# Column transforms in four array tiles at once, and a last stage with small chunks at both ends and four buffers

## The chip, the cores and the metric

The kernel runs on one core of a Trainium2 chip. A core has a tensor engine (PE; its weight loads are listed apart as PEld), a vector engine (DVE), a scalar engine (ACT), a general engine (POOL), a sync engine (SP) that here only issues transfers, and 16 DMA engines that move data between the device memory (HBM) and the on-chip buffer (SBUF). The tensor engine writes its results into PSUM, eight banks of 512 float32 values for each of 128 partitions; DVE and ACT copy ("evacuate") them to SBUF. The metric is the device time of one launch in microseconds. Before the change it is 1813.42 us, the median of three runs from 1812.36 to 1813.81. The profiled execution has a span of 1809.2 us, and all times of single instructions below are counted from its start.

## The reference, cut to what matters

The input is `x` of shape (4, 56, 56, 128), float32: four images of 3136 tokens with 128 channels. Layer 0 is a group norm, a 7x7 neighbourhood attention with four heads and a projection, added to `x`. Layer 1 adds an unnormalised attention over the tokens, and then a spectral unit: the normalised tokens are convolved along the sequence with 16 long filters (once plainly, once with alternating signs), and each filtered sequence goes through a 128x128 matrix of its own. Only one of four branches counts in the end, chosen by an argmax:

```
U = irfft(rfft(phi) * rfft(u))                  # 16 filters, plain and with signs
out = einsum('btkd,k,kde->bte', U, sigma**0.25, M)
t = t + out + (three short shifted products)
```

The change touches the way back from frequencies to tokens, and the sum into the output.

## The kernel before, in words

Everything is float32. `layers` does layer 0, layer 1's attention, the row half of the forward transform and the transforms of the filters; the change does not touch it. It leaves the current sum `t` in device memory as `td`, the row-transformed tokens as `xd`, and the filters' transforms as `vd`. A flag decides whether a second, general form of everything runs; with these inputs it does not.

`spectral_layer` then works frequency by frequency. The 3136 tokens are seen as a grid of 56 rows and 56 columns. The row transform gave N1 = 42 row frequencies `m1`; each holds a real and an imaginary part, two halves of the sequence (`NS` = 2, index `s`) and four images (`B`). Columns are split into even and odd ones (index `p`), so that a column transform is a product with a 56-row operand on partitions 0 to 55 for `p` = 0 and 64 to 119 for `p` = 1. The steps for one `m1` are:

- `token_points` (L1466): 16 products, 8 for each `p`, turn the tokens into 28 column frequencies, in one PSUM bank for each `p`: bank `px` of pool `ps_x`, and a bank of tag `g0`, shown as `xx`. DVE copies each bank to the tile `us` (L1481), ACT multiplies part of the same bank by -1 into `us` (L1482), POOL makes further copies (L1483 to L1485).
- `matrices` (L1487), eight calls `n` = 0 to 7: each fills four banks, `pg[0][0]`, `pg[0][1]`, `pg[1][0]`, `pg[1][1]`, of tags `g0`, `g1`, `g0`, `g1`, by 16 products of 32 rows. The four products of one round go to the four banks in this order. DVE evacuates the `g0` banks and ACT the `g1` banks into `gt` (L1505).
- `product` (L1510), seven calls: the frequency's tokens times its matrices, into `py`, evacuated as `ys`.
- `regroup` (L1524): `ys` goes to device memory as `yd` and comes back as `yg`, in the order that the inverse transform needs.
- `columns` (L1536): the inverse column transform, four products of 56x56 with 512 columns, one for each `s` and `p` (L1542). Each has a bank of its own, drawn in the order `g1`, `g0`, `g1`, `g0`. Four evacuations of 56x512 (L172 on ACT and L174 on DVE by turns) fill `zs`.
- `store_columns` (L1554): four transfers (L1556), one for each `p` and part, to `zd`, which is laid out column by column: `zd[w, part * 42 + m1, s, b, e]`.

The PSUM pool `ps_g` holds three banks for each of the tags `g0` and `g1`; a new tile of a tag takes one of its three banks, and the first instruction that writes it waits until the bank's last reader is done. The order of the tensor engine's instructions is as written (`manual_schedule`); the order on the other engines is picked by the framework's scheduler when the kernel is built. The loop runs `it` from -1 to 44 and works in a software pipeline: in pass `it` it interleaves `matrices` of frequency `it` with `product` of `it - 1`, and after the last of them come, in this order on the tensor engine, `token_points` of `it + 1` and `columns` of `it - 3`. Passes 3 to 40 (38 of them) have all four kinds of work.

`onto_the_rest` (L1600) is the last stage. For each of the 56 columns `w` it multiplies the 84 x 1024 values of `zd[w]` by a table `onto` (two accumulating products of 84x56 with 512 columns, L1625), multiplies by a mask and adds to `td` (DVE, L1634), and stores to the output. Columns `w` and `w + 28` (index `q`) go together, on the lower and upper half of the partitions. Seven chunks of `WC` = 4 column pairs are worked on, each with its transfers: `tl` from `td` (L1615, issued by ACT), `z` from `zd` (L1617, by SP, one for each `q`, 1344 KB), and the output (L1639, by ACT). The pool `fin` has three buffers of each, and its first transfers wait for the memory that the spectral pools give back. All `z` loads wait until the last `zd` store has landed, since every store touches every column.

Of the kernel before, what the change touches and what calls it, by code (L numbers as in the profile page):

```python
# [10 lines left out]
F32 = mybir.dt.float32  # L11
# [4 lines left out]
P = 128  # L16
B, H, W, C = 4, 56, 56, 128
# [39 lines left out]
NS, BR = 2, H // 2  # L57
N1, N2, NM = 42, W, W // 2
# [6 lines left out]
HALF = 2 * NM  # L65


def spectral_tables():

    m1 = np.arange(N1)  # L70
    m = m1[:, None] + N1 * np.arange(NM)[None]
    row = np.exp(-2j * np.pi * (m1[None] + 0.25) * np.arange(H)[:, None] / N1)
    rows = np.stack([row.real, row.imag], 1)
    into = np.zeros((P, 2 * N1))
    for g in range(NG):
        into[32 * g : 32 * g + BR] = rows[:BR].reshape(BR, -1)
    tok, back = np.zeros((2, N1, P, 2, NM))
    fil = np.zeros((N1, P, 2, NM, 2))
    for p in range(2):
        col = np.arange(p, N2, 2)  # L80

        fwd = np.exp(-2j * np.pi * (m[:, None, :] + 0.25) * col[None, :, None] / (2 * NP))

        bwd = np.exp(2j * np.pi * (m[:, :, None] + 0.25) * col[None, None, :] / (2 * NP)) / NP
        for part, turn in enumerate((1, 1j)):
            at = slice(64 * p + NM * part, 64 * p + NM * (part + 1))
            for to, a in ((tok, turn * fwd), (back, turn * bwd)):
                to[:, at] = np.stack([a.real, a.imag], 2)

            a = turn * fwd  # L90
            fil[:, 64 * part + NM * p : 64 * part + NM * (p + 1), p] = np.stack([a.real, a.imag], 3)

    onto = np.zeros((2, N1, NS, H))
    for s in range(NS):
        at = np.arange(H - BR * s)
        e = np.exp(2j * np.pi * (m1[:, None] + 0.25) * at[None] / N1)
        onto[0, :, s, BR * s :] = e.real
        onto[1, :, s, BR * s :] = -e.imag
    sign = np.ones((P, 1))
    sign[BR:N2] = sign[64 + BR : 64 + N2] = -1.0  # L100
    f = lambda a: np.ascontiguousarray(a, np.float32)
    return {
        "into": f(into),
        "taps_in": f(rows.reshape(H, -1)),
        "tok": f(tok.reshape(N1, P, -1).transpose(1, 0, 2)),
        "fil": f(fil.reshape(N1, P, -1).transpose(1, 0, 2)),
        "back": f(back.reshape(N1, P, -1).transpose(1, 0, 2)),
        "onto": f(onto.reshape(2 * N1, -1)),
        "sign": f(sign),
    }  # L110
# [13 lines left out]
def hybrid_kernel(  # L124
# [23 lines left out]
    nc = tc.nc  # L148
# [19 lines left out]
    def evacuate(dst, src):  # L168

        flip[0] ^= 1  # L170
        if flip[0]:
            nc.scalar.copy(dst, src)  # L172
        else:
            nc.vector.tensor_copy(dst, src)  # L174
# [1238 lines left out]
    def spectral_layer():  # L1413


        with ExitStack() as ph:
# [37 lines left out]
            def parts():  # L1454

                for p in range(2):
                    for part in range(2):
                        yield slice(64 * p + NM * part, 64 * p + NM * (part + 1)), p, part
# [77 lines left out]
            def columns(m1, yg, zs, pz):  # L1536

                back = tables_of(m1)[2]
                for s in range(NS):
                    for p in range(2):  # L1540
                        at = slice(64 * p, 64 * p + HALF)
                        nc.tensor.matmul(  # L1542
                            pz[s][p][at],
                            back[at],
                            yg[at, s * B : (s + 1) * B].rearrange("p k e -> p (k e)"),
                            start=True,
                            stop=True,
                        )
                for s in range(NS):
                    for p in range(2):  # L1550
                        at = slice(64 * p, 64 * p + HALF)
                        evacuate(zs[at, s], pz[s][p][at])

            def store_columns(m1, zs):  # L1554
                for at, p, part in parts():
                    nc.sync.dma_start(  # L1556
                        zd[p::2, part * N1 + m1].rearrange("w s b e -> w (s b e)"),
                        zs[at].rearrange("w s f -> w (s f)"),
                    )

            def bank(tag):
                if tag == "x":
# [6 lines left out]
            with tc.manual_schedule(engines={mybir.EngineType.PE}):  # L1569
                for it in range(-1, N1 + LAG):  # L1570
                    ap, az, au = it - 1, it - LAG, it + 1
                    if 0 <= it < N1:
                        gts[it] = sp.tile([P, 2, 2 * NM, C // 2, 2], F32, name="gt")
                        if it + 2 < N1:
                            xms[it + 2] = load_tokens(it + 2)
                    if 0 <= ap < N1:
                        ys = sp.tile([P, NM // 4, C], F32, name="ys")
                    if 0 <= az < N1:
                        zs = sp.tile([P, NS, B * C], F32, name="zs")
                    for n in range(8):  # L1580
                        if 0 <= it < N1:
                            matrices(it, gts[it], n)
                        if 0 <= ap < N1 and n < 7:
                            if n % 4 == 0:
                                py = ps_y.tile([P, 4, C], F32, name="py")
                            product(py, gts[ap], us2[ap % 2], n)
                            if n == 3 or n == 6:
                                evacuate(ys[:, n - n % 4 : n + 1], py[:, : n % 4 + 1])
                    if au < N1:
                        token_points(au, xms.pop(au), us2[au % 2], [bank("x"), bank("g0")])  # L1590
                    if 0 <= az < N1:
                        pz = [[bank(f"g{1 - p}") for p in range(2)] for s in range(NS)]
                        columns(az, ygs.pop(az), zs, pz)
                    if 0 <= ap < N1:
                        ygs[ap] = regroup(ap, ys)
                    if 0 <= az < N1:
                        store_columns(az, zs)
                    gts.pop(ap, None)

    def onto_the_rest():  # L1600

        with ExitStack() as ph:
            fin = ph.enter_context(tc.tile_pool(name="fin", bufs=3))
            ps_o = ph.enter_context(tc.tile_pool(name="ps_o", bufs=4, space=bass.MemoryType.PSUM))
            onto = fin.tile([2 * N1, NS, H], F32, name="onto", bufs=1)
            nc.sync.dma_start(onto, table["onto"].rearrange("p (s h) -> p s h", s=NS))
            rows_in = td.rearrange("b (h w) c -> h b w c", w=W)
            rows_out = ot.rearrange("b (h w) c -> h b w c", w=W)
            WC = 4
            for w0 in range(0, W // 2, WC):  # L1610
                tl = fin.tile([P, B, WC, C], F32, name="tl")
                zin = []
                for q in range(2):
                    ws = slice(q * BR + w0, q * BR + w0 + WC)
                    nc.scalar.dma_start(tl[64 * q : 64 * q + H], rows_in[:, :, ws])  # L1615
                    z = fin.tile([2 * N1, WC, NS, B * C], F32, tag=f"z{q}", name=f"z{q}")
                    nc.sync.dma_start(  # L1617
                        z, zd[ws].rearrange("w p s b e -> p w s (b e)")
                    )
                    zin.append(z)  # L1620
                for i in range(WC):
                    po = ps_o.tile([P, B, C], F32, name="po2")
                    for s in range(NS):
                        for q in range(2):
                            nc.tensor.matmul(  # L1625
                                po[64 * q : 64 * q + H].rearrange("p b c -> p (b c)"),
                                onto[:, s],
                                zin[q][:, i, s],
                                start=(s == 0),
                                stop=(s == NS - 1),  # L1630
                            )
                    for q in range(2):
                        at = slice(64 * q, 64 * q + H)
                        nc.vector.scalar_tensor_tensor(  # L1634
                            tl[at, :, i], po[at], hmask[at], tl[at, :, i], ALU.mult, ALU.add
                        )
                for q in range(2):
                    ws = slice(q * BR + w0, q * BR + w0 + WC)
                    nc.scalar.dma_start(rows_out[:, :, ws], tl[64 * q : 64 * q + H])  # L1639

    unfit = keep.tile([1, 1], mybir.dt.int32, name="unfit")
    layers(False, unfit)
# [61 lines left out]
```

## Time and profile before

| what | us |
| --- | --- |
| time, median of three | 1813.42 |
| span of the profile | 1809.2 |
| `layers` until the first token product (L1472) | 0 to 779.1 |
| spectral loop, first to last column evacuation's end | 779.1 to 1656.2 |
| one pass of the loop in its steady part (n = 0 of two passes: 1007.02 and 1027.35) | 20.33 |
| last stage, first `z` issue to the end | 1659.1 to 1809.2 |
| PE busy / DVE busy / ACT busy over the span | 1657.9 / 1070.5 / 756.3 |

A busy tensor engine in this profile is not one at its peak: matmuls are pipelined, their ends are modelled, and a short wait between two of them can be covered by the modelled end of the first. What a pass costs is therefore read from start times. In the slices of the page each digit is the busy share of one fortieth of the span, 45.2 us; the last three and a bit are the last stage, and the nineteen before them the loop.

### The profile page before, as it was taken

Reading aid. Unit: us, or ns where it says so; the run is one execution under the profiler, and the core shown is the slowest. Engines: PE = TensorE matmul, PEld = TensorE weight load, DVE = VectorE, ACT = ScalarE, POOL = GpSimd, SP = SyncE. Lnnn points to the kernel's source line nnn. Section 1 sums busy time; section 2 is a strip of 40 time slices with the busy share of each in tenths; the row PEclk is TensorE's granted clock in tenths of the full one; section 3 lists DMA queues with packets and bytes.
Section 4 is the critical chain, followed back from the end, with each engine's and each line's share of the span. In section 5 each row is a group of like instructions: output and inputs, shape, how many; then the busy total and the mean of one; then the engine's idle time right before and its main releaser. Section 6 shows DMA issues by size and latency. Waiting matters only on the chain. (4 is left out here: it accounts for less than half of the span.)

```text
span 1809.2 us, 71326 instructions
## 1 busy us (share of the span) xinstructions
PE 1657.9 (92%) x31481; PEld 1237.5 (68%) x31481; DVE 1070.5 (59%) x2142; ACT 756.3 (42%) x1529; POOL 390.3 (22%) x803
## 2 busy tenths in 40 slices
PE   4887898899999998779999999999999999995997
PEld 3665677567867766368888887888888887883221
DVE  4776786678868764135666666565666666562232
ACT  2333533366455444324444544454444544451000
POOL 4242254437446434000010001000000001000000
PEclk9788989899999997659999999999999999997555
DMA  6545446544343334632333333433434333325996
GB/s 166 116 88 106 86 94 147 121 119 124 88 136 91 92 98 112 198 92 65 99 106 105 96 87 100 113 99 88 102 104 107 89 91 97 103 72 150 239 226 182
DMA packets 285099, 207.69 MB, mean 115 GB/s; under 512 B 105868, under 2 KB 255532, under 8 KB 284652
## 3 DMA queue, kind: packets, MB, share of 16 engines
q1 hardware_dynamic: 275876, 189.50, 41.1%
q10 hardware_dynamic: 8904, 13.53, 2.7%
q8 instruction: 250, 4.10, 1.0%
q14 instruction: 69, 0.57, 0.1%
HBM read 115.31 MB, written 87.64 MB: 112 GB/s over the span
## 5 line engine op out<-in xcount | busy, mean ns | idle before, releaser
L1505 DVE COPY gt<-pg 128x448 f32<-128x448 f32 x672 | 388.4, 619 | 303.3 <-PE pg L1495 303.3
L1505 ACT COPY gt<-pg 128x448 f32<-128x448 f32 x672 | 326.0, 538 | 358.1 <-PE pg L1495 358.1
L1495 PE MATMUL pg<-v,mats 32*128 32x112 f32 x10752 | 402.2, 286 | 5.6 <-DVE gt L1505 2.0
L1495 PEld LDWEIGHTS pg<-v,mats 32*128 32x128 f32 x10752 | 341.8, 190 | 93.3 <-issue 51.7
L1514 PE MATMUL py<-gt,us 128*32 128x128 f32 x9408 | 339.2, 283 | 0.8 <-ACT ys L172 0.8
L1514 PEld LDWEIGHTS py<-gt,us 128*32 128x32 f32 x9408 | 266.9, 137 | 32.9 <-ACT ys L172 1.0
L1484 POOL COPY us<-us 128x448 f32<-128x448 f32 x42 | 23.4, 556 | 819.7 <-DVE us L1481 819.7
L1165 ACT ACTIVATE e<-scores 126x768 f32<-126x768 f32 (+1 forms) x140 | 107.3, 767 | 117.6 <-PE scores L1149 91.7
L1169 DVE TENSOR_TENSOR e<-e,relb 126x768 f32<-126x768 f32 (+1 forms) x140 | 137.9, 986 | 28.8 <-ACT e L1165 28.2
L1625 PE MATMUL po<-z,onto 84*56 84x512 f32 x224 | 124.8, 1067 | 20.8 <-DMA tl<-td 16.0
L1193 DVE RECIPROCAL recs<-results 128x96 f32<-128x96 f32 (+1 forms) x140 | 99.5, 711 | 49.4 <-PE results L1179 48.5
L1149 PE MATMUL scores<-qT,kp 32*126 32x96 f32 (+1 forms) x2240 | 105.0, 300 | 7.9 <-ACT e L1165 7.4
L1149 PEld LDWEIGHTS scores<-qT,kp 32*126 32x126 f32 (+1 forms) x2240 | 81.4, 196 | 43.9 <-ACT e L1165 17.9
L1625 PEld LDWEIGHTS po<-z,onto 84*56 84x56 f32 x224 | 31.8, 207 | 113.8 <-issue 98.1
L1634 DVE SCALAR_TENSOR_TENSOR tl<-po,hmask,tl 56x512 f32<-56x512 f32 x56 | 42.0, 750 | 104.4 <-PE po L1625 103.8
L1472 PE MATMUL px<-tok,xm 56*128 56x56 f32 x672 | 86.8, 281 | 18.1 <-DMA v<-vd 18.1
L1472 PEld LDWEIGHTS px<-tok,xm 56*128 56x128 f32 x672 | 81.3, 194 | 24.2 <-issue 19.9
L1179 PE MATMUL results<-e,v_sb 126*32 126x96 f32 (+1 forms) x2240 | 78.7, 261 | 11.7 <-DVE aT L1194 10.2
L1542 PE MATMUL xx<-yg,back 56*56 56x512 f32 x336 | 83.5, 611 | 4.0 <-DMA yg<-yd 4.0
L1472 PE MATMUL xx<-tok,xm 56*128 56x56 f32 x672 | 86.9, 281 | 0.0
L812 PE MATMUL bk<-mu,ut 128*112 128x128 f32 x672 | 81.8, 279 | 3.5 <-POOL ut L798 1.5
L812 PEld LDWEIGHTS bk<-mu,ut 128*112 128x112 f32 x672 | 77.0, 185 | 7.0 <-POOL ut L798 1.7
(177 smaller groups left out, 2106.1 us busy)
## 6 DMA issues: line engine op xcount, KB each, us to landing
xd<-xs SPq DMA_DIRECT2D x112, 168.0 KB
xm<-xd SPq DMA_DIRECT2D x168, 112.0 KB
yd<-ys SPq DMA_DIRECT2D x168, 112.0 KB
yg<-yd SPq DMA_DIRECT2D x168, 112.0 KB
zd<-zs SPq DMA_DIRECT2D x168, 112.0 KB
z<-zd SPq DMA_DIRECT2D x14, 1344.0 KB
v_sb<-vpad SPq DMA_DIRECT2D x224, 63.0 KB
acc<-in_x_dram SPq DMA_DIRECT2D x28, 224.0 KB
```

The source lines that it names most:

```text
L812: nc.tensor.matmul(pt[:CP, g * C : (g + 1) * C], ut[:, t0 : t0 + 2 * CP - 1 : 2], mu[:, i, :], start=(i == 0), stop=(i == NAR - 1),)
L1149: nc.tensor.matmul(sp[:, h, c * nq : (c + 1) * nq], keys_of(x0, y0 + c * KH, KH)[hs], qTs[b, ty][hs, QR * x0 : QR * x0 + nq], start=True, ...
L1165: nc.scalar.activation(e.rearrange("k (h q) -> k h q", h=NH), sp, AF.Exp)
L1169: nc.vector.tensor_tensor(e, e, relb[qc].rearrange("k h c q -> k (h c q)"), ALU.mult)
L1179: nc.tensor.matmul(po[hs, i, :nq], ones[:kn] if i else v_sb[:kn, c, hs], e[:, h, c], start=(c == 0), stop=(c == 1),)
L1193: nc.vector.reciprocal(rec, po[:, 1, :nq])
L1472: nc.tensor.matmul(pu[p][:, HALF * k : HALF * (k + 1)], xm[at, k // B, k % B, :], tok[at], start=True, stop=True,)
L1495: nc.tensor.matmul(pg[g // 2][g % 2][:, 4 * NM * i : 4 * NM * (i + 1)], mats[rows, 4 * n + i, :], v[rows], start=True, stop=True,)
L1505: copy(gt[:, h, :, e0 : e0 + 4, :], pg[q][h][:, : 16 * NM].rearrange("p (i m c) -> p m i c", i=4, c=2),)
L1514: nc.tensor.matmul(py[32 * j : 32 * (j + 1), n % 4, :], us.rearrange("p c k m -> p (c k) m")[:, NSB * FIRST[p, c] : NSB * (FIRST[p, c] + 4 ...
L1542: nc.tensor.matmul(pz[s][p][at], back[at], yg[at, s * B : (s + 1) * B].rearrange("p k e -> p (k e)"), start=True, stop=True,)
L1625: nc.tensor.matmul(po[64 * q : 64 * q + H].rearrange("p b c -> p (b c)"), onto[:, s], zin[q][:, i, s], start=(s == 0), stop=(s == NS - 1),)
```

## The change

Two parts.

First, the inverse column transform. The table `back` is padded with zeros from 56 to 64 columns, so that a product fills 64 partitions of its output. The four products of a frequency then go to two banks instead of four: bank `p` takes `s` = 0 on partitions 0 to 63 and `s` = 1 on partitions 64 to 127. The operand's partitions (64 times `p`) and the output's (64 times `s`) put each product into its own 64x64 quarter of the array. Each bank is evacuated by one copy of 128x512, in place of two of 56x512. `zs` now has `s` on its partitions and `p` in its rows, so the four stores are one for each `s` and part, of 2 KB runs instead of 4 KB.

Second, the last stage. The chunks have 1, 1, 2, 4, 4, 4, 4, 4, 2, 1, 1 column pairs instead of seven times 4; the pool has four buffers instead of three, and its tiles wait for the single tiles whose memory they take over (`reuse_waits="tile"`); the table `onto` is loaded on ACT's queue and no longer on SP's. The aim is to start the tensor engine sooner after the first transfer, and to leave less work after the last one.

```
-    tok, back = np.zeros((2, N1, P, 2, NM))
+    tok = np.zeros((N1, P, HALF))
+    back = np.zeros((N1, P, 64))
...
                     for p in range(2):
                         at = slice(64 * p, 64 * p + HALF)
                         nc.tensor.matmul(
-                            pz[s][p][at],
+                            pz[p][64 * s : 64 * (s + 1)],
                             back[at],
                             yg[at, s * B : (s + 1) * B].rearrange("p k e -> p (k e)"),
                             start=True,
                             stop=True,
                         )
+                for p in range(2):
+                    evacuate(zs[:, p], pz[p])
+
+            def store_columns(m1, zs):
+                to = zd.rearrange("(c p) r s b e -> c p r s (b e)", p=2)
                 for s in range(NS):
-                    for p in range(2):
-                        at = slice(64 * p, 64 * p + HALF)
-                        evacuate(zs[at, s], pz[s][p][at])
-
-            def store_columns(m1, zs):
-                for at, p, part in parts():
-                    nc.sync.dma_start(
-                        zd[p::2, part * N1 + m1].rearrange("w s b e -> w (s b e)"),
-                        zs[at].rearrange("w s f -> w (s f)"),
-                    )
+                    for part in range(2):
+                        at = 64 * s + NM * part
+                        nc.sync.dma_start(to[:, :, part * N1 + m1, s], zs[at : at + NM])
...
-                        pz = [[bank(f"g{1 - p}") for p in range(2)] for s in range(NS)]
+                        pz = [bank("g1"), bank("g0")]
...
-            fin = ph.enter_context(tc.tile_pool(name="fin", bufs=3))
+            fin = ph.enter_context(tc.tile_pool(name="fin", bufs=4, reuse_waits="tile"))
...
-            nc.sync.dma_start(onto, table["onto"].rearrange("p (s h) -> p s h", s=NS))
+            nc.scalar.dma_start(onto, table["onto"].rearrange("p (s h) -> p s h", s=NS))
...
-            WC = 4
-            for w0 in range(0, W // 2, WC):
-                tl = fin.tile([P, B, WC, C], F32, name="tl")
+
+            steps = (1, 1, 2, 4, 4, 4, 4, 4, 2, 1, 1)
+            assert sum(steps) == W // 2
+            for n, wc in enumerate(steps):
+                w0 = sum(steps[:n])
+                tl = fin.tile([P, B, max(steps), C], F32, name="tl")
...
-                    nc.scalar.dma_start(tl[64 * q : 64 * q + H], rows_in[:, :, ws])
-                    z = fin.tile([2 * N1, WC, NS, B * C], F32, tag=f"z{q}", name=f"z{q}")
+                    nc.scalar.dma_start(tl[64 * q : 64 * q + H, :, :wc], rows_in[:, :, ws])
+                    z = fin.tile([2 * N1, max(steps), NS, B * C], F32, tag=f"z{q}", name=f"z{q}")
                     nc.sync.dma_start(
-                        z, zd[ws].rearrange("w p s b e -> p w s (b e)")
+                        z[:, :wc], zd[ws].rearrange("w p s b e -> p w s (b e)")
                     )
...
-                for i in range(WC):
+                for i in range(wc):
...
-                    nc.scalar.dma_start(rows_out[:, :, ws], tl[64 * q : 64 * q + H])
+                    nc.scalar.dma_start(rows_out[:, :, ws], tl[64 * q : 64 * q + H, :, :wc])
```

More of the change, by code (lines that the diff above doesn't have):

```diff
@@ L87, in spectral_tables @@
             for to, a in ((tok, turn * fwd), (back, turn * bwd)):
-                to[:, at] = np.stack([a.real, a.imag], 2)
+                to[:, at, :HALF] = np.concatenate([a.real, a.imag], 2)
             a = turn * fwd
@@ L104, in spectral_tables @@
         "taps_in": f(rows.reshape(H, -1)),
-        "tok": f(tok.reshape(N1, P, -1).transpose(1, 0, 2)),
+        "tok": f(tok.transpose(1, 0, 2)),
         "fil": f(fil.reshape(N1, P, -1).transpose(1, 0, 2)),
-        "back": f(back.reshape(N1, P, -1).transpose(1, 0, 2)),
+        "back": f(back.transpose(1, 0, 2)),
         "onto": f(onto.reshape(2 * N1, -1)),
@@ L1578, in spectral_layer @@
                     if 0 <= az < N1:
-                        zs = sp.tile([P, NS, B * C], F32, name="zs")
+                        zs = sp.tile([P, 2, B * C], F32, name="zs")
                     for n in range(8):
@@ L1602, in onto_the_rest @@
         with ExitStack() as ph:
-            fin = ph.enter_context(tc.tile_pool(name="fin", bufs=3))
+            fin = ph.enter_context(tc.tile_pool(name="fin", bufs=4, reuse_waits="tile"))
             ps_o = ph.enter_context(tc.tile_pool(name="ps_o", bufs=4, space=bass.MemoryType.PSUM))
             onto = fin.tile([2 * N1, NS, H], F32, name="onto", bufs=1)
-            nc.sync.dma_start(onto, table["onto"].rearrange("p (s h) -> p s h", s=NS))
+            nc.scalar.dma_start(onto, table["onto"].rearrange("p (s h) -> p s h", s=NS))
             rows_in = td.rearrange("b (h w) c -> h b w c", w=W)
             rows_out = ot.rearrange("b (h w) c -> h b w c", w=W)
-            WC = 4
-            for w0 in range(0, W // 2, WC):
-                tl = fin.tile([P, B, WC, C], F32, name="tl")
+            steps = (1, 1, 2, 4, 4, 4, 4, 4, 2, 1, 1)
[3 more added lines that the diff above has]
+                tl = fin.tile([P, B, max(steps), C], F32, name="tl")
                 zin = []
                 for q in range(2):
-                    ws = slice(q * BR + w0, q * BR + w0 + WC)
-                    nc.scalar.dma_start(tl[64 * q : 64 * q + H], rows_in[:, :, ws])
-                    z = fin.tile([2 * N1, WC, NS, B * C], F32, tag=f"z{q}", name=f"z{q}")
+                    ws = slice(q * BR + w0, q * BR + w0 + wc)
+                    nc.scalar.dma_start(tl[64 * q : 64 * q + H, :, :wc], rows_in[:, :, ws])
+                    z = fin.tile([2 * N1, max(steps), NS, B * C], F32, tag=f"z{q}", name=f"z{q}")
                     nc.sync.dma_start(
-                        z, zd[ws].rearrange("w p s b e -> p w s (b e)")
+                        z[:, :wc], zd[ws].rearrange("w p s b e -> p w s (b e)")
                     )
                     zin.append(z)
-                for i in range(WC):
+                for i in range(wc):
                     po = ps_o.tile([P, B, C], F32, name="po2")
@@ L1637, in onto_the_rest @@
                 for q in range(2):
-                    ws = slice(q * BR + w0, q * BR + w0 + WC)
-                    nc.scalar.dma_start(rows_out[:, :, ws], tl[64 * q : 64 * q + H])
+                    ws = slice(q * BR + w0, q * BR + w0 + wc)
+                    nc.scalar.dma_start(rows_out[:, :, ws], tl[64 * q : 64 * q + H, :, :wc])
     unfit = keep.tile([1, 1], mybir.dt.int32, name="unfit")
```

## The prediction

> **What bounds the kernel now.** I read the page's slices first, then windows, then the waits, then the timeline of one pass engine by engine, then the chain that ended last.
>
> ```profile
> PE   4887898899999998779999999999999999995997
> DMA  6545446544343334632333333433434333325996
> ```
>
> PE fills the loop (slices 18 to 36) with DMA at 2 to 4 tenths. In the last stage (slices 37 to 40) DMA rises to 9, then falls to 6 at the very end. The windows sharpen this (columns: window, length, busy of PE, PEld, DVE, ACT, POOL, granted clock, DMA share, GB/s):
>
> ```profile
> 1500.00:1600.00 100.00, 99.56 (x2564) 81.59 (x2561) 60.35 (x103) 49.01 (x103) 8.22 (x15) 1.00 0.35 91
> ...
> 1700.00:1710.00 10.00, 10.00 (x22) 2.69 (x20) 3.48 (x5) 0.00 (x0) 0.00 (x0) 0.50 0.89 280
> ...
> 1790.00:1800.00 10.00, 10.00 (x18) 2.48 (x15) 4.50 (x6) 0.00 (x0) 0.00 (x0) 0.50 0.17 58
> ```
>
> The loop looks bound by PE. The last stage is bound by DMA at a share near 0.9 until about 1790; after it the last chunk's products, at half the clock, run alone. A PE at 99.56 of 100 us could still wait, since modelled ends cover waits; so I looked at the waits of the weight loads:
>
> ```profile
> ACT us L1482 <- DVE us L1481: 94.9, 46, 21.7
> ...
> PEld pg L1495 <- ACT us L1482: 37.4, 38, 1.3
> ```
>
> 38 times, once for each full pass, the first `matrices` product waits for ACT's L1482, about 1 us each. The timeline of one pass shows why (start, duration, engine, line):
>
> ```profile
> 1005.00 1.93 PE L1542 MATMUL xx<-yg,back 56*56 56x512 f32 x8
> 1007.02 1.24 PE L1495 MATMUL pg<-v,mats 32*128 32x112 f32 x32
> ```
> ```profile
> 1005.17 0.62 DVE L1481 COPY us<-px 128x448 f32<-128x448 f32 x1 [0.85 <-PE xx L1472]
> 1005.72 0.61 DVE L1481 COPY us<-xx 128x448 f32<-128x448 f32 x1
> ```
> ```profile
> 1005.89 0.36 ACT L1482 ACTIVATE us<-px 128x224 f32<-128x224 f32 x1 [1.72 <-DVE us L1481]
> 1006.14 0.57 ACT L172 COPY zs<-xx 56x512 f32<-56x512 f32 x1
> 1006.61 0.36 ACT L1482 ACTIVATE us<-xx 128x224 f32<-128x224 f32 x1
> ```
>
> The token products end near 1005.07. Then a chain runs outside PE: DVE reads bank `px`, DVE reads bank `xx`, ACT reads `xx` until 1006.97, and at 1007.02 PE starts `matrices`, whose first `g0` bank is that `xx`. `columns`, from 1005.00, lies beside this chain and hides it almost exactly. **PE's real cost for `columns` is thus hidden time: what it gives back is mostly filled by the chain.** A pass ahead of the first `columns` shows the chain with nothing of `zs` on ACT:
>
> ```profile
> 826.10 1.16 PE L1495 MATMUL pg<-v,mats 32*128 32x112 f32 x32
> ...
> 826.81 0.61 DVE L1481 COPY us<-xx 128x448 f32<-128x448 f32 x1
> ...
> 827.52 0.36 ACT L1482 ACTIVATE us<-xx 128x224 f32<-128x224 f32 x1 [0.17 <-DVE us L1481]
> ```
>
> Here PE goes on at once, as only three `g0` banks were drawn from n = 7 to n = 0 and `xx` is not needed yet; and ACT's second read starts 0.71 us after DVE's second copy.
>
> ```profile
> 1787.07 13.92 PE po L1625 x24
> ...
> 1801.79 0.76 DVE tl L1634
> ```
>
> The chain that ended last: the last chunk's 16 products, its DVE work, then the output's transfer, to 1809.2.
>
> **What the skill says.** (1) The Trainium skill, TensorEngine Tiling (Array Packing), "Tiling Modes": 64x64 gives four independent tiles that load and multiply in parallel. The trace agrees for its neighbours: L1472's two row tiles start 10 ns apart, L1495 runs four row tiles and L1514 four column tiles; four quarters at once it does not show. (2) TensorE: Matmul & The Clock Gate, Part 3: matmuls start and end in program order, so one that waits for a bank holds all behind it. The trace agrees: no later product passes L1495 while it waits. (3) PSUM — Partial Sum Buffer, "PSUM bank collisions": two engines may not use one bank and quadrant at once, so ACT's read of `xx` comes after DVE's; the 94.9 us above are that. (4) DMA: Bandwidth & Descriptors, "Why a DMA increments its semaphore by 16": a transfer uses the largest number of engines up to 16 that divides its slowest dimensions. For 84 and 56 rows that is 14 of 16, 0.875; the 0.89 to 0.91 measured fit, so the stage is at its ceiling, and chunk size does not change it.
>
> **Part 1, `columns`.** Eight records of 589 ns take 1.93 us: four rounds of two, a round of (1.93 - 0.59)/3 = 0.45. Four quarters at once make two rounds: 0.45 + 0.59 = 1.04, or PE free about 0.9 us sooner. Bounds: no more than pairs (gain 0) and all of it (0.9). I take four at once.
> Then the banks. Per pass `g0` is drawn by `matrices` n = 7 (two: A, B), `token_points` (C), `columns` (now only A), and n = 0 (B, then C). `g1` has slack. So the first two products of n = 0 go to free banks, and the third needs C, the `xx` bank: the same chain. Any of the three that n = 0 could have is either C or the one `columns` just filled, which DVE frees later still (1006.36 + 0.69 = 1007.05).
> When is C free? Without a `zs` copy ahead on ACT: 1005.72 + 0.71 + 0.36 + 0.05 = 1006.84. With it still ahead (one copy of about 0.585, by `ys` 128x512, ready at about 1006.04): as now, 1007.03. The third product now starts two places after 1007.02, at 16 products in 1.09 us (n = 0 to 7 repeat) 0.14 later, 1007.16. The gain is 0.32 or 0.13 a pass. The scheduler's order on ACT isn't to be seen; I take the middle, 0.23. 38 passes: **8.7 us**, bounds 5 and 12.
> Costed at nothing: one copy less on DVE (0.69) and on ACT (0.57), both 50 to 60% busy; 2 KB runs in the `zd` stores, at a DMA share of 0.35; stores that wait for both copies, behind which SP's `yg` loads queue, needed only two passes later; 8 more columns of `back` to load (127 ns a load now).
> The loop's end: the last `columns` runs from 1650.69 to 1655.4 at the low clock with `zs` waiting 6.3 us for a buffer; the copies end at 1656.2 and the stores land by 1658.8. One copy for each engine instead of two takes out about 0.7; with the earlier end of pass 41's `columns` **1.5 us**, bounds 0 and 3.
>
> **Part 2, the last stage.** Bytes: `z` 14 x 1.376 = 19.3 MB, `tl` and output 14 x 0.459 = 6.4 MB each, 32.1 in all. From 1659.1 until the last chunk's PE start at 1787.07 came all `z`, all `tl` and five of seven outputs, 30.3 MB: 0.237 MB/us. A smaller first chunk starts PE at about 1665 instead of 1671, but DMA is the bound there and works either way: worth nothing alone, except that outputs can start earlier. A smaller last chunk cuts the end: now 1809.2 - 1787.1 = 22.1 us after the last `z`; of PE 13.9.
> After, bound by DMA: 32.1/0.237 = 135.4 us. 512 byte packets: the loop's queue took 36.1% of 16 engines in 600 us, 3466 us, for 9912 packets of 4 KB (0.25 us by the last stage's first 36 us), 26880 of 512 B and 8666 smaller (0.02 at most): 0.03 for 512 B, against 0.11/4 = 0.0275 in a 2 KB one. Four single pairs have 3584 of them: under 1 us on 14 engines; with 1 KB ones I take 1.5. A `tl` issued before the last `zd` store lands takes off about 1. Then 2 for the receipt and 3 in which DMA idles behind the last pair: 1659.1 + 135.4 + 1.5 - 1 + 5 = 1800.
> After, bound by PE's tail: chunks of 4, 2, 1, 1 stand at the end. The eighth `z` (24 of 28 pairs) is complete after 16.5 + 6.4 + 3.7 = 26.6 MB, 112 us, at 1771; then 8 pairs at 13.65/4 = 3.41 us, 27.3, DVE 1.5 and a last small output of 3.7 (6.6 now, with 0.9 MB): 1804. The fourth buffer lets `z` run ahead and lowers that by some us. I take 1801.7: **7.5 us**, bounds 2 and 13.
>
> Sum: 8.7 + 1.5 + 7.5 = 17.7, so 1813.4 - 17.7 = 1795.7; I say **1795.5**.
>
> **Rivals.** (a) The bank chain does not bind (PE finds other banks, or the chain gets shorter than I think). Then a pass gains the whole 0.9 or a bit more: 38 x 0.95 = 36, total 45: 1768. For: the pass at 826 goes on without a wait. Against: there `columns` drew no bank. (b) PE gains nothing in the loop, for want of quarters or because the zs copy stays ahead and the third bank is drawn first, and PE's tail takes the last stage: gains 0 + 1 + 5: 1807. (c) Slower: quarters do not run at once, the merged bank is full only at 1006.9, and ACT's order stays `px`, `zs`, `xx`; then C is free at about 1006.9 + 0.58 + 0.36 = 1007.85 instead of 1007.02, 0.7 x 38 = 26 lost, less 9 from the rest: 1830. Against: L1495 and L1514 show four tiles of both kinds at once.
>
> **Numbers.** Forecast 0.70, (a) 0.08, (b) 0.14, (c) 0.08. Range: the forecast's bounds are 1785 to 1806.5, and (b) lies at their upper edge: 1784 to 1807. Faster by over 0.2% (3.6 us) 0.89, within 0.2% 0.04, slower 0.07.
>
> **What would show it.** L1542's eight records in about 1.05 us. The third product of n = 0 waiting for L1482, n = 0 to n = 0 at about 20.1 us instead of 20.33; 19.4 would be (a), 21 (c). ACT's order of L172 and the second L1482. DMA share at 0.9 to about 1785 of the old clock and from last `z` to the end some 10 us instead of 22. Wrong would be: `zs` copies delaying L1482, or small chunks that lower the DMA share.

## The result, and the profile after

The changed kernel takes 1792.53 us, the median of four runs from 1792.17 to 1796.78, against 1812.89 (1807.94 to 1813.81) for the kernel before in the same comparison. The ratio is 0.9899, with a 95% interval of 0.9875 to 0.9922: 14 to 23 us less. The forecast was 1795.5, with a range of 1784 to 1807.

The profiled execution of the changed kernel is its slowest, 1796.8 (span 1795.0), so single stages are compared here by their own start and end, not by the span. `layers`, which has not changed, ended at 779.1 before, at 777.8 after, and at 772.5 in one of the experiments: some us of a span are not the edit's.

| stage, us | before | after | difference |
| --- | --- | --- | --- |
| one full pass | 20.33 | 20.12 | -0.21, in 38 passes -8.0 |
| first column product to the last evacuation's end | 862.7 to 1656.15 | 861.0 to 1645.34 | -9.1 |
| last evacuation's end to the first `z` issue | 2.99 | 5.14 | +2.15 |
| first `z` issue to the end | 150.1 | 144.5 | -5.6 |

The sum of the last three is -12.5; `layers` gives the rest of this pair of spans (-14.2). The page's slices keep their picture, a loop filled by PE and a last stage filled by DMA:

```profile
PE   4787888899999998869999999999999999995898
DMA  6544456544343334642333433433333433335986
```

One pass of the changed kernel, PE first, then DVE and ACT (start, duration, engine, line; the line numbers are one higher than before):

```profile
1001.86 1.09 PE L1543 MATMUL xx<-yg,back 56*64 56x512 f32 x8
1002.88 0.48 PE L1496 MATMUL pg<-v,mats 32*128 32x112 f32 x4
1003.69 1.15 PE L1496 MATMUL pg<-v,mats 32*128 32x112 f32 x28 [0.33 <-ACT us L1483]
```
```profile
1002.57 0.61 DVE L1482 COPY us<-xx 128x448 f32<-128x448 f32 x1
1003.11 0.69 DVE L175 COPY zs<-xx 128x512 f32<-128x512 f32 x1
```
```profile
1002.75 0.36 ACT L1483 ACTIVATE us<-px 128x224 f32<-128x224 f32 x1 [1.72 <-DVE us L1482]
1003.28 0.36 ACT L1483 ACTIVATE us<-xx 128x224 f32<-128x224 f32 x1 [0.17 <-DVE us L1482]
1003.80 0.59 ACT L173 COPY zs<-xx 128x512 f32<-128x512 f32 x1 [0.16 <-DMA yd<-ys]
```

The eight records of `columns` take 1.09 us instead of 1.93: all four quarters run at once. Then four records, which are the first two products of n = 0 (a product shows as two), and a hole until ACT has read bank `xx` (1003.28 + 0.36). The other 28 records, from the third product on, start 1.83 us after `columns`; before, the third would have started 2.16 after. On ACT the second L1483 now stands ahead of the `zs` copy. The waits say the same, twice per full pass (us in total, times, longest):

```profile
PEld pg L1496 <- DVE us L1482: 30.8, 38, 0.8
PEld pg L1496 <- ACT us L1483: 19.4, 38, 0.5
PE pg L1496 <- ACT us L1483: 12.7, 38, 0.3
```

At the loop's end the stores of `zs`, first those of before and then those of after (minimum, median, maximum of the issue in ns; first and last start in us):

```profile
L1556 SPq DMA_DIRECT2D zd<-zs x168: 306/384/1798, 865.2 to 1656.5; - x168
```
```profile
L1558 SPq DMA_DIRECT2D zd<-zs x168: 788/837/1932, 863.3 to 1647.9; - x168
```

A store of 56 runs of 2 KB takes SP twice as long to issue as one of 28 runs of 4 KB. The last four now stand between the last evacuation and the first `z`. Before, it was two: a store then held the columns of one `p`, and the two of `p` = 0 were issued ahead of the last evacuation. The last issue ended 0.76 us after that evacuation before, and ends 3.36 us after it now. At the old 0.31 to 0.38 us each, four issues in a row would take about 1.5 (an estimate), so some 0.7 of these 2.6 us come from stores that wait for both copies, and the rest from the longer issue. The last stage ends in this chain (start, duration, what):

```profile
1760.24 27.57 PE po L1627 x56
1787.84 0.75 DVE tl L1636
1788.61 0.76 DVE tl L1636
```

After the last 4-pair chunk has arrived, PE works for 27.57 us without a break. The windows (length; busy of PE, PEld, DVE, ACT, POOL; clock, DMA share, GB/s) show that DMA runs out of work towards the end of it:

```profile
1770.00:1780.00 10.00, 10.00 (x26) 2.86 (x24) 4.50 (x6) 0.00 (x0) 0.00 (x0) 0.50 0.88 281
1780.00:1790.00 10.00, 7.80 (x16) 1.75 (x12) 4.50 (x6) 0.00 (x0) 0.00 (x0) 0.50 0.47 143
```

### The profile page after: what moved, and what is told of

Its sections match the earlier page's. It is cut to its first block, busy times and chain, and to the rows that moved or that the text cites. A ratio compares the mean times of both kernels' runs of the same rounds, so it can differ in the third digit from the quotient of the medians.

```text
span 1795.0 us, 71349 instructions
## 1 busy us (share of the span) xinstructions
PE 1632.6 (91%) x31481; PEld 1235.4 (69%) x31481; DVE 1036.9 (58%) x2100; ACT 737.4 (41%) x1487; POOL 391.7 (22%) x803
## 4 chain that ended last, share of the span: by engine, by line
PE 67%; DMA 13%; DVE 7%; POOL 5%; SPq 4%; issue 2%; ACT 2%; DVEq 0%; ACTq 0%; POOLq 0%
PE pg L1496 21%; PE py L1515 18%; PE px L1473 4%; PE results L1180 4%; PE scores L1150 3%; PE bk L878 3%; DMA z<-zd 3%; SPq L220 3%; PE po L1627 3%; DMA m_raw<-in_M_minus_dram 2%; PE xx L1543 2%; PE bk L813 2%; DMA out_dram<-tl 2%; POOL v L520 2%; DMA vpad<-vt 2%
## 5 line engine op out<-in xcount | busy, mean ns | idle before, releaser
L1496 PE MATMUL pg<-v,mats 32*128 32x112 f32 x10752 | 416.7, 286 | 14.6 <-ACT us L1483 12.7
L1496 PEld LDWEIGHTS pg<-v,mats 32*128 32x128 f32 x10752 | 349.5, 190 | 106.6 <-issue 48.5
L1180 PEld LDWEIGHTS results<-e,v_sb 126*32 126x32 f32 (+1 forms) x2240 | 47.8, 114 | 48.9 <-DVE aT L1195 26.3
```

The costliest lines, as they stand in the source:

```text
L1180: nc.tensor.matmul(po[hs, i, :nq], ones[:kn] if i else v_sb[:kn, c, hs], e[:, h, c], start=(c == 0), stop=(c == 1),)
L1496: nc.tensor.matmul(pg[g // 2][g % 2][:, 4 * NM * i : 4 * NM * (i + 1)], mats[rows, 4 * n + i, :], v[rows], start=True, stop=True,)
```

## The experiments

Times are medians; ratios are against the kernel before on the same chip, with their 95% intervals. "Tail" is the time from the last evacuation's end to the end of the span.

### One part at a time

`e1_cols_only` has the edit of `columns`, `store_columns` and the tables alone; `e2_last_only` has that of `onto_the_rest` alone.

> The kernel before with the column transforms changed and the old last stage. Theory (the bank chain sets the pass, the last stage is a separate gain): a pass of 20.12 us as in the changed kernel, 8.5 us less in the loop, and no more than that: about 1804 to 1806. The stores of 2 KB runs cost 0.8 us each on SP instead of 0.4, so that from the last evacuation to the first z issue it takes about 4.6 to 5.1 us instead of 3.0. Rival (the whole 20 us come from the columns): about 1793.

> The kernel before with the new last stage and the old columns. Theory: the last stage takes about 144.5 us from the first z issue as in the changed kernel, instead of 150.1, and the wait for the last zd store stays near 3 us: 6 to 8 us less, 1805 to 1807. Rival (tl loads that start early slow the last zd stores, and not their shorter runs): from the last evacuation to the first z issue about 5 us here too.

| run | time | ratio | pass | last evacuation to first `z` | tail |
| --- | --- | --- | --- | --- | --- |
| before | | | 20.33 | 2.99 | 153.0 |
| changed | 1792.53 | 0.9899 (0.9875 to 0.9922) | 20.12 | 5.14 | 149.7 |
| e1, columns | 1799.65 | 0.9957 (0.9942 to 0.9973) | 20.12 | 5.60 | 156.0 |
| e2, last stage | 1799.20 | 0.9959 (0.9943 to 0.9975) | 20.33 | 1.62 | 144.6 |

In us these are -7.8 and -7.4 against that comparison's 1806.64; together -15.2, inside the interval of the whole change. The absolute times that were expected are missed by 4 to 8 us, as the kernel before ran faster on that chip; the differences fit. The longer wait before `z` comes with the columns: 5.6 in e1, which has the old last stage, against 3.0 before. So the new stores cost 2.6 us at the loop's end.

The 1.6 of e2 does not compare with these. It was said above that every store touches every column; that is true of the changed kernel alone. In the old layout a store holds even or odd columns, and the first two `z` of e2 (columns 0 and 28, one each) need the even ones only: they are issued 1.62 and 1.97 us after the last evacuation, and the third (column 1) 3.27 after it, against 2.99 for the first `z` before. The early `tl` loads thus delay the landing of the stores by little here, and the rival that blamed them falls for these chunk sizes. Together the two parts lose what e2 had: in the changed kernel the first small chunk has to wait for all four stores. The tails fit this: +3.0 for e1 and -8.4 for e2 against the kernel before, but -3.3 and not -5.4 for both.

### The bank chain: the order on PE

```
-                    if au < N1:
-                        token_points(au, xms.pop(au), us2[au % 2], [bank("x"), bank("g0")])
                     if 0 <= az < N1:
                         pz = ...
                         columns(az, ygs.pop(az), zs, pz)
+                    if au < N1:
+                        token_points(au, xms.pop(au), us2[au % 2], [bank("x"), bank("g0")])
```

The same move in the changed kernel (e3) and in the kernel before (e4).

> The changed kernel with columns written ahead of token_points in each pass. Theory (PE waits 0.7 us in each full pass for the xx bank behind DVE and ACT): now token_points covers the evacuation of the columns' bank, n = 0 finds both of its g0 banks free, and a pass falls from 20.12 to about 19.4 us; 38 passes give 27 us, so about 1766. Rival (the pass is bound by PE's own work, and the gain in the loop came from fewer evacuations): a pass stays at 20.1, time 1792.

> The kernel before with columns written ahead of token_points. Theory: with pairs of columns the chain was almost hidden, so there is only the wait of about 0.16 us to be had: a pass of about 20.2 instead of 20.33, 5 to 6 us less, 1807. Against the changed kernel with the same order (19.4 a pass) this shows what four array quarters save when nothing hides it: about 0.8 us a pass. Rival (order matters for another reason, such as earlier loads): the same step as in the changed kernel, 0.7 us a pass, 1786.

e3: 1764.15 us, ratio 0.9751 (0.9712 to 0.9789). e4: 1799.68 us, ratio 0.9957 (0.9946 to 0.9968). A pass is 19.32 us in e3 and 20.12 in e4, by the starts of n = 0; e3 first, then e4:

```profile
1014.17 1.09 PE L1543 MATMUL xx<-yg,back 56*64 56x512 f32 x8
1017.11 1.16 PE L1496 MATMUL pg<-v,mats 32*128 32x112 f32 x32
...
1036.43 1.16 PE L1496 MATMUL pg<-v,mats 32*128 32x112 f32 x32
```
```profile
1014.32 1.93 PE L1542 MATMUL xx<-yg,back 56*56 56x512 f32 x8
1018.10 1.16 PE L1495 MATMUL pg<-v,mats 32*128 32x112 f32 x32
...
1038.22 1.16 PE L1495 MATMUL pg<-v,mats 32*128 32x112 f32 x32
```

In both, n = 0 runs through as one group of 32 records, and of the 38 waits for L1482 or L1483 none is left in e3 and one of 0.2 us in e4. The `g0` bank that the third product of n = 0 takes is now the one of `columns`, which is evacuated while `token_points` runs; the bank `xx` is not drawn again before n = 1. This is the answer to what the array's quarters are worth: 0.80 us a pass (20.12 against 19.32) where nothing else ends later, and only 0.21 (20.33 against 20.12) where the bank's release does. The order's own part is 0.21 in the kernel before and 0.80 in the changed one.

### The bank chain: one link taken out

```
-                    nc.scalar.mul(us[:, 6 + 2 * p], src[:, 1], -1.0)
+                    nc.scalar.mul(us[:, 6 + 2 * p], us[:, 2 * p + 1], -1.0)
```

> The changed kernel with ACT's multiplication by -1 reading DVE's copy in us instead of the PSUM bank, so that the bank is free when DVE's second copy ends. Order on PE as in the changed kernel. Theory: the third product of n = 0 comes 0.46 us sooner (ACT's 0.36 and its hand-over are off the chain); a pass falls from 20.12 to about 19.65, 38 passes give 17 us, so about 1775 against 1792. Rival (the order of columns and token_points matters for another reason than the bank): a pass stays at 20.1.

1776.03 us, ratio 0.9813 (0.9784 to 0.9842). The waits for an engine that are left at `matrices` are those for DVE alone (this run, passes from 900 to 1590 us):

```profile
PEld pg L1496 <- DVE us L1482: 29.2, 36, 0.8
```
```profile
1018.77 1.53 PE L1496 MATMUL pg<-v,mats 32*128 32x112 f32 x32
```

A pass is 19.63 us (n = 0 at 1018.77 and 1038.40). ACT's link cost 0.49 a pass, against 0.46 expected. PE's order is that of the changed kernel, so it is the bank and not the order as such. The rest of the chain, DVE's second copy, still costs 0.31 (19.63 against 19.32): the group of n = 0 takes 1.53 us and not the 1.16 of e3, and its third product starts at 1019.15, 0.05 after that copy's end. The listed 0.8 us lie beside `columns` and cost nothing: n = 0 starts 1.02 after `columns` here, and in e3 `token_points` does so too.

### The last stage, edit by edit

e6 is the changed kernel with `steps = (4, 4, 4, 4, 4, 4, 4)`; e7 has `steps = (4, 4, 4, 4, 4, 4, 2, 1, 1)`.

> The changed kernel with seven chunks of 4 column pairs and still four buffers. Theory (the small last chunks make the gain of the last stage): 149 to 151 us from the first z issue to the end, as before; the time 5 to 6 us above the changed kernel. Rival (the fourth buffer makes it): 144 to 145, as with the small chunks.

> The changed kernel with chunks of 4 at the start and 4, 2, 1, 1 at the end. Theory (the start is bound by transfers, so small first chunks are worth nothing): 143 to 145.5 us from the first z issue to the end, the same as the changed kernel. Rival (a sooner first product counts): some 6 us more.

1794.64 us, ratio 0.9911 (0.9885 to 0.9938), tail 152.1 for e6; 1793.18, 0.9903 (0.9881 to 0.9925), tail 150.1 for e7. My theory that the small last chunks make the gain falls: against e1, which has the old last stage and a tail of 156.0, the even chunks already have 3.9 of the 6.3 us. The small end brings 2.0 more and the small start 0.4, each within what the tail varies by with one and the same last stage: 149.7 in the changed kernel, and 148.9, 147.4 and 148.3 in the runs e3, e5 and e8. The measure of e6's expectation, from the first `z` issue, reads 143.0 and misleads. Its first `z` comes 9.1 us after the last evacuation instead of 5.6, because the `tl` loads of whole chunks get in between (5.3 in e10 below, where they wait for the pools), so part of the transfers lies ahead of it; the tail counts that.

Which edit, then? e9 is e6 with three buffers, e10 is e6 with the pool's old kind of waits:

```
-            fin = ph.enter_context(tc.tile_pool(name="fin", bufs=4, reuse_waits="tile"))
+            fin = ph.enter_context(tc.tile_pool(name="fin", bufs=3, reuse_waits="tile"))     # e9
+            fin = ph.enter_context(tc.tile_pool(name="fin", bufs=4))                         # e10
```

> The kernel of the even chunks with three buffers instead of four, and its tiles still waiting for single tiles of the spectral pools. From the last evacuation to the end it took 156.0 us with three buffers and waits for the pools (the run with the columns alone) and 152.1 with four and single tiles. Theory (the fourth buffer lets z run ahead of the products): about 155 here. Rival (the tl loads that start beside the last zd stores make the gain): about 152 to 153.

> Even chunks with four buffers and waits for the spectral pools as before. Theory (the fourth buffer makes the gain): about 152 to 153 us from the last evacuation to the end. Rival (the early tl loads): about 156.

| run | buffers | waits for | time | ratio | tail | fifth chunk, us after the last evacuation | from there to the end |
| --- | --- | --- | --- | --- | --- | --- | --- |
| e1 | 3 | pools | 1799.65 | 0.9957 (0.9942 to 0.9973) | 156.0 | 98.7 | 57.3 |
| e9 | 3 | single tiles | 1799.27 | 0.9954 (0.9943 to 0.9965) | 157.7 | 99.2 | 58.6 |
| e10 | 4 | pools | 1799.72 | 0.9953 (0.9937 to 0.9968) | 156.3 | 103.6 | 52.7 |
| e6 | 4 | single tiles | 1794.64 | 0.9911 (0.9885 to 0.9938) | 152.1 | 99.1 | 53.0 |

(In e1 `onto` is also loaded on SP's queue.) Neither is worth anything alone; together they are worth 0.4% in time, measured on different chips and with intervals that just touch for e6 and e10. The last two columns take DVE's first work on a chunk as its start, and show what each edit does. The fourth buffer shortens the last three chunks by about 5 us; with waits for the pools it also starts the fifth chunk 5 us later, which uses that up. The early loads with four buffers take this delay away: DMA's share is 0.43 from 1644 to 1650 in e10, and 0.82 from 1642 to 1651 in e6. That both edits are needed is measured; why the early loads bring nothing with three buffers was not settled.

The tensor engine does not set the end here, though a line of e6 looks like it. First PE's last run of products in e6, then DVE's work at the two chunk boundaries inside it:

```profile
1737.73 48.62 PE L1627 MATMUL po<-z,onto 84*56 84x512 f32 x88 [0.34 <-DMA z<-zd]
```
```profile
1751.67 1.53 DVE L1636 SCALAR_TENSOR_TENSOR tl<-po,hmask,tl 56x512 f32<-56x512 f32 x2 [1.90 <-PE po L1627]
1758.73 1.53 DVE L1636 SCALAR_TENSOR_TENSOR tl<-po,hmask,tl 56x512 f32<-56x512 f32 x2 [5.53 <-PE po L1627]
...
1768.97 1.53 DVE L1636 SCALAR_TENSOR_TENSOR tl<-po,hmask,tl 56x512 f32<-56x512 f32 x2 [1.90 <-PE po L1627]
1776.15 1.53 DVE L1636 SCALAR_TENSOR_TENSOR tl<-po,hmask,tl 56x512 f32<-56x512 f32 x2 [5.65 <-PE po L1627]
```

DVE follows the products of a column pair, and pairs without a wait come 3.41 us apart. At the boundaries they are 7.06 and 7.18 apart, so PE waited some 3.7 us at each, and the modelled ends of the products hide it.

DVE's first work on the last chunk is at 1776.15 in e6, 1773.99 in e9 and 1781.92 in e10. From there to the end it takes 18.3 us in all three runs. What differs is when that chunk can start: 133.8 us after the last evacuation in e6, 139.4 in e9, 138.0 in e10. Each time its second `z` landed 3.7 us earlier (130.1, 135.7, 134.3 by the semaphore times of the traces). So the arrival of the last `z` sets the end with even chunks, with three buffers and with four.

### Tries at a better kernel

e8 is e3 with two of the last frequency's four stores issued by ACT. e11 is e3 with `steps = (1, 1, 2, 4, 4, 4, 4, 2, 2, 2, 1, 1)`. e12 is e3 with `steps = (1, 1) + (2,) * 12 + (1, 1)` and `bufs=8`, which takes the memory of four buffers of 4.

> Columns ahead of token_points, and of the last frequency's four stores two are issued by ACT. Theory (four stores at 0.8 us each on one queue make the wait for the first z): from the last evacuation to the first z issue about 1.6 us less than the 5.5 without it, so about 3.9, and the time 1 to 2 us lower than 1764. Rival (the landing takes the time, whatever the queue): the wait stays above 5.

> Columns ahead of token_points, and the last chunk of 4 split into 2 and 2. Theory (after the eighth z the tensor engine has 8 pairs of 3.41 us left, and only the arrival of that chunk of 4 holds it up): the engine starts on the first two pairs about 5 us sooner, and from the last evacuation to the end it takes 144 to 146 us instead of 148.8; time about 1760. Rival (the output transfers set the end by then): 148 to 149, time 1764.

> Columns ahead of token_points, chunks of 1, 1, then 2, and 1, 1 at the end, with eight buffers of half the size. Theory (tensor engine's tail as in the run with the split chunk, and tl packets of 1 KB instead of 2 KB cost transfer time): 144 to 148 us from the last evacuation to the end. Rival (small packets cost more than the tail gives back): above 149.

e8: 1764.66 us, ratio 0.9759 (0.9737 to 0.9782). The wait for the first `z` fell from 5.55 to 4.63 and not to 3.9, since ACT takes 2.48 us for its two issues, and the time did not fall. e11: 1761.79 us, ratio 0.9753 (0.9715 to 0.979), tail 151.8; nothing won, and the tail is worse. A likely reason is that a chunk of 2 in a buffer made for 4 halves what is loaded ahead. The chain that ended last goes through outputs, then `tl`, then `z`:

```profile
1706.85 11.73 DMA out_dram<-tl
1719.04 11.02 DMA tl<-td
1730.12 7.93 DMA z<-zd
1738.09 13.92 PE po L1627 x28
```

With the depth in bytes kept (e12) the tail falls to 143.9 against e3's 148.9, by more than the 2.3 us that it varies by: 1756.80 us, ratio 0.9728 (0.969 to 0.9767). In time this is not clear of noise, since e3's interval (0.9712 to 0.9789) overlaps. From 1620 to 1740 its DMA share is 0.91 to 0.93, and the products behind the last wait take 13.9 us. In e3 they take some 27: its last run in the trace is 78.9 us long, but DVE's work comes every 3.41 us only for the last eight pairs, from 1732.44 on. e12 has the lowest median of the kernels, 51 us below the kernel before on the same chip (1807.74).

## Why the prediction was right, point by point

**The bound of the loop.** Right, and the runs show it: a release chain of DVE, DVE and ACT holds the third product of n = 0 in the changed kernel. Taking out ACT's link gave 0.49 us a pass, and a change of order 0.80.

**The quarters.** Forecast 1.04 us for the eight records, measured 1.09.

**The pass.** Forecast a gain of 0.23, as the middle of 0.13 and 0.32; measured 0.21. The middle was near for a wrong reason. ACT's order turned out to be the favourable one, and the third product came 1.83 us after the start of `columns`, as worked out (1.84). But the step to "0.32 a pass" fails by 0.11: after the wait the fourteen remaining products need 1.08 us where sixteen needed 1.17 before, so about 0.05 of the two early products is lost, and the rest of the pass took 0.06 longer. The 0.06 lie in the `product` groups n = 1 and n = 2, which take 1.10 us each from start to start instead of 1.07 (means of 34 passes); why is open.

**The loop's end.** Forecast 1.5 us won; measured about 1.5 lost. The evacuation came 0.6 earlier, counted from the third last `columns` (21.84 instead of 22.47), but two terms of "costed at nothing" were wrong there, the "2 KB runs in the `zd` stores" and the "stores that wait for both copies". In the passes no engine is seen to wait for them; at the loop's end four issues of 0.79 to 0.80 us, instead of two of 0.31 and 0.38, stand behind the last evacuation. The wait rose from 3.0 to 5.1.

**The last stage.** Forecast 7.5 us; measured 5.6 in this pair of profiles, 7.1 in e2 (150.1 against 143.0). Of the two bounds, the one by PE's tail was the right one: the eighth `z` complete 112 us after the first issue (109.8 measured), then 27.3 us of products (27.57 measured), and an end 145 us after the first issue (144.5). The last output took 5.6 us from the end of DVE's work and not 3.7. Where the gain came from was wrong: "a smaller last chunk cuts the end" holds only 2 us of it. The fourth buffer and the early `tl` loads, which the forecast put at "some us" and "about 1", bring about 4 together and none apart. The estimate of the transfers rested on a share at its ceiling, 14 of 16 engines or 0.875, that chunk size does not change: the shares measured lie above this (0.89 to 0.91), and e12 with its chunks of 2 has 0.91 to 0.93, so that ceiling is not what the traces show.

**The rivals.** (a), no wait at the bank, is what the changed order reaches and the change itself does not. (b), nothing gained in the loop, and (c), pairs only, are excluded by the 1.09 us and the pass of 20.12.

**The sum.** Here luck had a part. The errors at the loop's end (3 us) and in the last stage (2 us) both made the forecast too favourable: against 17.7 forecast, the stages of the pair of profiles sum to 12.5, their spans differ by 14.2, and e1 and e2 add up to 15.2. That the medians differ by 20.4 is not explained by the stages; the kernel before alone ran from 1807.94 to 1813.81.

**A reading.** The 94.9 us that ACT's L1482 waits for DVE were read as the price of a shared bank. In a full pass that wait is 1.72 us ahead of ACT's read of `px`, and about half of it passes before the token products end. What binds is the second read, of `xx`. That it comes after DVE's copy is shown by the traces; why it does is not.

## What to carry to other kernels

Before an operation of the busiest engine is made shorter, look for what waits for a bank right after it: here about three quarters of 0.80 us went into a release chain that had been hidden, and the full amount came back by putting `columns`, whose bank is free after one copy, ahead of `token_points`, whose bank has several readers: the bank that is slow to come free is then drawn again later. If chunks are made small, smaller and more buffers keep what is loaded ahead the same in bytes; e12 did better with this than e11 without it. A store with twice as many runs cost nothing that the passes show inside this loop, and it was on the path at the loop's end. A long run of products in a profile may have waits in it; the engine that evacuates them shows the true spacing.

## What the runs showed of the hardware

Four products of 56x64 with 512 float32 columns, one in each quarter of the array, take 1.09 us together; in pairs they take 1.93. A store's issue on SP takes 0.38 us with 28 runs and 0.84 with 56, at equal bytes (medians). In the last stage of the changed kernel the granted clock was 0.50 in every window, also from 1770 to 1780, within the 27.57 us in which products ran without a break.
